# Second batch's attention residual: added by an accumulating load instead of by VectorE

## The chip, the cores and the metric

The kernel runs on one core of one Trainium2 chip. The metric is device time in microseconds for one execution. A core has five engines that each work through their own queue in order and wait for one another by semaphores: TensorE (PE; its weight loads are shown as PEld), VectorE (DVE), ScalarE (ACT), GpSimd (POOL) and SyncE (SP). Transfers are issued from the SP, ACT and GpSimd queues and carried out by 16 DMA engines.

## The reference

Input x is (4 batches, 512 times, 128 features f, 64 channels h), float32; d = f * h = 8192. Layer 0, cut to its formulas:

```python
xn = layernorm(x.reshape(b, t, d), ln_attn_g, ln_attn_b)
k, v, r = xn @ Wk, xn @ Wv, sigmoid(xn @ Wr)          # 64 states each
states = scan over t of  s = decay * s + k_t * v_t
x = x + ((r * states) @ Wo).reshape(b, t, f, h)       # attention, its residual
xn = layernorm(x.reshape(b, t, d), ln_freq_g, ln_freq_b).reshape(b, t, f, h)
x = x + gelu(convolution over f of xn, 3 taps, h -> h, + freq_b)
xn = layernorm(x.reshape(b, t, d), ln_time_g, ln_time_b)
to = causal depthwise convolution over t of xn, 3 taps, + time_b
x = x + layernorm(to, time_ln_g, time_ln_b)
x = x + gelu(x @ ffn_W1 + ffn_b1) @ ffn_W2 + ffn_b2   # over h
```

Layer 1 takes a moving average over t (25 wide) as trend, transforms the rest over t, mixes 128 modes by complex weights per channel, transforms back and adds the trend. The change touches the lines of the attention and the convolution over f alone, and for one of the four batches.

## The kernel before

Layer 0 keeps one batch as 64 chunks of 128 rows of d (two f times 64 h) by 512 times. Two chunks make a pair, so a batch has 32 pairs (`NPR`), and a pair is a tile of 128 partitions by 2 x 512 float32, 512 KB. Five stages run for each batch: `project` (k, v, r and the statistics of the first layernorm), `scan`, `attend_and_convolve`, `convolve_time`, and `feed_forward`.

TensorE's order is written by hand: each stage is a generator that issues a piece and yields its weight, and `in_turn` steps two generators alternately by their share of progress. Its table puts the attention and convolution over f of batch 1 beside the convolution over t of batch 0. The other engines' orders come from the framework's scheduler, which also sets the semaphore waits; every queue is then in order. A tile from a pool is a rotating buffer: a new tile of a tag waits until the old holder's readers are done.

`attend_and_convolve(b)` works by pairs in a loop over i. Step i does these pieces:

- `attend(i)`: SP loads the pair of x into xp (L295, in `load_x`) and a block of Wo (L525). TensorE multiplies Wo by r * states into the one PSUM tile of tag "a" (L529). VectorE adds xp to it, which gives x1 (L531, 3 buffers of tag "x1"), and multiplies x1 by the second layernorm's scale, which gives z (L535, 4 buffers).
- `convolve(i - 2)`: TensorE starts with the constant part (L550), then the neighbouring chunks of z (L559; so it needs z of the pair after it), then the chunks themselves (L564). ScalarE applies gelu in PSUM (L565), VectorE adds x1, which gives x2 (L567), GpSimd issues the store of x2 to memory (L568), ScalarE squares x2 (L570) and makes the convolution's weights two pairs ahead (L543).
- `add_up(i - 3)`: TensorE sums x2 and its square over d (L252, into st), for the third layernorm.

`convolve_time(0)`, which runs beside it, takes per pair: a load of x2 from SP (L612), VectorE's multiply and subtract (L613, L616), on ScalarE the first tap of two chunks (L621), on VectorE the four other taps (L625), on GpSimd a correction of two columns (L631) and the store of the result (L632), on ScalarE its square (L672), on TensorE the sums (L252, into p).

Tags "xp" and "x1" have three buffers each. `spare(tag, n)` gives a tile of a tag in the same pool.

Of the kernel before, what the change touches and what calls it, by code (L numbers as in the profile page):

```python
# [10 lines left out]
F32 = mybir.dt.float32  # L11
AF = mybir.ActivationFunctionType
ALU = mybir.AluOpType
# [3 lines left out]
P = 128  # L17
# [5 lines left out]
SL = 512  # L23
NS = D // SL
NPR = NCH // 2
# [55 lines left out]
def layer0(ctx, tc, dram, x, xt, vecs, wkvr, wo, wdec, wconv, fbias, w1, fb1, w2, fb2, x4):  # L81
# [4 lines left out]
    nc = tc.nc  # L86
# [7 lines left out]
    fr = ctx.enter_context(tc.tile_pool(name="fr", bufs=3))  # L94
# [10 lines left out]
    def two(pool, tag):  # L105
        return pool.tile([P, 2, SL], F32, tag=tag, name=tag)
# [54 lines left out]
    def neighbours(q, c):  # L161

        return (c - 1, q), (c + 1, 1 - q)

    def rows_of(q, d):

        return 1 - q if d < 0 else q
# [79 lines left out]
    def add_up(st, i, pair, squares, first, last):  # L247

        for j in range(2):
            for k, src in ((0, pair), (1, squares)):  # L250
                q = 2 * j + k
                nc.tensor.matmul(  # L252
                    st[32 * q : 32 * q + 32, :], lhsT=ones, rhs=src[:, j, :],
                    start=first, stop=last,
                )

    def finish(st, bank, tag):

        s_sb = rowp.tile([P, SL], F32, tag="s", name="s_sb")
        nc.scalar.copy(s_sb, st)  # L260
        yield CHAIN
        pm = bank()
        for t in range(NT):
            nc.tensor.matmul(
                pm[:, 2 * t : 2 * t + 2], lhsT=s_sb[:, t * P : (t + 1) * P], rhs=pick,
                start=True, stop=True,
            )
        me = tiny.tile([P, NT, 2], F32, tag=f"me{tag}", name="me")
        nc.vector.tensor_copy(me.rearrange("p t k -> p (t k)"), pm[:, 0 : 2 * NT])
        return me[:, :, 0], me[:, :, 1]  # L270

    def moments(mean, square, tag):

        var, rs, mrs = cols(f"var{tag}"), cols(f"rs{tag}"), cols(f"mrs{tag}")
        nc.vector.tensor_tensor(var, mean, mean, ALU.mult)
        nc.vector.tensor_tensor(var, square, var, ALU.subtract)
        rsqrt(rs, var)
        nc.vector.tensor_tensor(mrs, mean, rs, ALU.mult)
        return rs, mrs

    def rows(bank, a, b, names):
        both = rowp.tile([P, 2, SL], F32, tag=names, name=names)
        for k, col in enumerate((a, b)):
            pb = bank()
            spread(pb, col)
            nc.scalar.copy(both[:, k, :], pb)  # L286
            yield CHAIN
        return both[:, 0, :], both[:, 1, :]

    def pair_of(row):  # L290
        return row.unsqueeze(1).to_broadcast([P, 2, SL])

    def load_x(b, i):
        xp = fr.tile([P, 2, SL], F32, tag="xp", name="xp")
        nc.sync.dma_start(xp, xt[b, 2 * i : 2 * i + 2].rearrange("c p t -> p c t"))  # L295
        return xp

    def spare(tag, n):
        return fr.tile([P, 2, n], F32, tag=tag, name=tag, bufs={"z": 4, "wx": 2}.get(tag, 3))

    def c_bank():
        return two(ps_c, "c")
# [212 lines left out]
    def attend_and_convolve(b):  # L515
        rst, rs, mrs = scanned.pop(b)
        rb, mb = yield from rows(of_a, rs, mrs, "rm4" if b == 1 else "rm")

        nc.vector.tensor_scalar(mb, mb, at_one[:, 1:2], at_one[:, 0:1], ALU.mult, ALU.add)
        x1s, zs, ws, waiting = {}, {}, {}, {}  # L520

        def attend(i):
            xp = load_x(b, i)
            wo_sb = fr.tile([P, P], F32, tag="wo", name="wo_sb")
            nc.sync.dma_start(wo_sb, wo[:, i, :])  # L525
            at = two(ps_a, "a")
            for j in range(2):
                js = slice(j * S, (j + 1) * S)
                nc.tensor.matmul(at[:, j, :], lhsT=wo_sb[js, :], rhs=rst[js, :], start=True, stop=True)  # L529
            x1 = x1s[i] = fr.tile([P, 2, SL], F32, tag="x1", name="x1")  # L530
            nc.vector.tensor_tensor(x1, at, xp, ALU.add)  # L531
            z = fr.tile([P, 2, SL], F32, tag="z", name="z", bufs=4)
            for j in range(2):
                zs[2 * i + j] = z[:, j, :]
            nc.vector.tensor_tensor(z, x1, pair_of(rb), ALU.mult)  # L535

        def scaled(i):

            wcs = fr.tile([P, 2, P + H], F32, tag="wcs", name="wcs")
            for j in range(2):  # L540
                c = 2 * i + j
                ws[c] = wcs[:, j, :]
                nc.scalar.mul(wcs[:, j, :], wc_sb[:, i % 2, :], vec[:, G2, c : c + 1])  # L543

        def convolve(i):
            cv = c_bank() if i % 2 or held[0] else two(ps_m, "m")
            for h in range(2):
                for j in range(2):
                    q = 32 * (2 * h + j)
                    nc.tensor.matmul(  # L550
                        cv[h * H : (h + 1) * H, j, :], lhsT=cgr[q : q + 2, i, :], rhs=mb[q : q + 2, :],
                        start=True, stop=False,
                    )
            for j in range(2):
                c = 2 * i + j
                for n, h in neighbours(i % 2, c):
                    if 0 <= n < NCH:
                        rs = halves[rows_of(n // 2 % 2, n - c)]
                        nc.tensor.matmul(  # L559
                            cv[halves[h], j, :], lhsT=ws[n][rs, P:], rhs=zs[n][rs, :], start=False, stop=False  # L560
                        )
            for j in range(2):
                c = 2 * i + j
                nc.tensor.matmul(cv[:, j, :], lhsT=ws[c][:, 0:P], rhs=zs[c], start=False, stop=True)  # L564
            nc.scalar.activation(cv, cv, AF.Gelu_apprx_tanh)  # L565
            x2 = two(bk, "x2")
            nc.vector.tensor_tensor(x2, cv, x1s.pop(i), ALU.add)  # L567
            nc.gpsimd.dma_start(x2d[b][2 * i : 2 * i + 2].rearrange("c p t -> p c t"), x2)  # L568
            sq2 = bk.tile([P, 2, SL], F32, tag="sq", name="sq2")
            nc.scalar.activation(sq2, x2, AF.Square)  # L570
            for c in (2 * i - 2, 2 * i - 1):
                zs.pop(c, None)
                ws.pop(c, None)
            if i + 2 < NPR:
                scaled(i + 2)
            waiting[i] = x2, sq2

        for i in range(NPR + 3):

            while begin[attend_and_convolve] < b + (min(i, 3) - 3) / 4:  # L580
                yield BLOCKED
            if i < 2:
                scaled(i)
            if i < NPR:
                attend(i)
                yield 1.0
            if 1 < i < NPR + 2:
                convolve(i - 2)
                yield 5.0
            while i == 3 and feeding[0]:  # L590
                yield BLOCKED
            if i == 3:
                st = ps_s.tile([P, SL], F32, tag="s", name="st")
                free_s[0] = False
            if i > 2:
                add_up(st, i - 3, *waiting.pop(i - 3), i == 3, i == NPR + 2)
                yield 1.0
            if b == 0 and i >= NPR and i < NPR + 2:
                begin[attend_and_convolve] = b + (0.25 if i == NPR else 0.75)
        begin[attend_and_convolve], free_s[0] = b + 1, True  # L600
        mean3, sq3 = yield from finish(st, of_a, 3)
        carried[b] = moments(mean3, sq3, 3)
# [248 lines left out]
    def nothing(b):  # L851
        yield 1.0

    J, Z, A, C, O, F = project, scan, attend_and_convolve, convolve_time, open_feed, feed_forward
    begin[A] = 0
    needed = {A: scanned, C: carried, O: causal, F: opened}
# [340 lines left out]
```

## Time and profile before

| | us |
|---|---|
| median of 3 runs | 3745.81 (3739.15 to 3752.97) |
| the profiled execution | 3734.79 |
| its span, first to last instruction | 3733.0 |

Busy time over the span: PE 3521.2 us (94%), DVE 2671.9 (72%), ACT 1778.0 (48%), POOL 447.3 (12%). The shares differ by stage. Three stretches ahead of the stage that the change touches, from the same view:

| stretch, us | what runs | PE | DVE | ACT | POOL | DMA share |
|---|---|---|---|---|---|---|
| 200 to 300 | batch 0 attention, batch 1 project | 94.7 | 53.4 | 24.2 | 6.6 | 0.70 |
| 300 to 400 | the same | 97.7 | 53.4 | 29.7 | 8.0 | 0.73 |
| 400 to 511 | its end, with batch 1's scan | 106.5 | 63.6 | 45.3 | 12.2 | 0.55 |

In the profile a line reads: engine, line of the kernel, operation, tile written <- tiles read, shape. "Idle before" is time in which an engine waited, with what ended the wait. The time from issue to landing of a transfer is given for those from GpSimd. TensorE's ends are modelled, so a busy TensorE is not one at its peak.

### The profile page before, as it was taken

What the parts mean: (1) busy time and instruction counts of PE and PEld (TensorE: products, weight loads), DVE (VectorE), ACT (ScalarE), POOL (GpSimd) and SP (SyncE); (2) the same over time, 40 slices, a digit from 0 to 9 for tenths busy, and PEclk for the clock granted to TensorE, in tenths of its full rate; (3) what the DMA queues carried; (4) which work ended last, traced back from release to release, by engine and by line L of the source; (5) the groups of instructions that cost most, each with busy time, mean ns of one, the idle gap of its engine ahead of it and who ended that gap; (6) DMA issues with size and microseconds to landing.
All of it is one profiled execution on the core that took longest, in us unless ns stands there. A gap on an engine that the chain in (4) does not pass through costs nothing. (4 is left out here: it accounts for less than half of the span.)

```text
span 3733.0 us, 53000 instructions
## 1 busy us (share of the span) xinstructions
PE 3521.2 (94%) x20041; PEld 1360.6 (36%) x20041; DVE 2671.9 (72%) x3498; ACT 1778.0 (48%) x2331; POOL 447.3 (12%) x654
## 2 busy tenths in 40 slices
PE   9999999999998999999989989999989999989998
PEld 4433322234333223433322233333323843328533
DVE  4455569976776896676789699946658277792677
ACT  0012346655656565565656578868854200152100
POOL 0000012210101221001122122100000000001000
PEclk9999999999999999999999999999999999999999
DMA  9867657787874687788578677645569478894687
GB/s 314 279 211 242 227 177 262 260 276 265 290 262 168 235 280 271 266 292 278 182 238 286 213 247 267 234 149 196 198 203 287 150 240 290 290 297 164 213 294 260
DMA packets 427223, 910.29 MB, mean 244 GB/s; under 512 B 32728, under 2 KB 83160, under 8 KB 422872
## 3 DMA queue, kind: packets, MB, share of 16 engines
q1 hardware_dynamic: 353136, 636.92, 52.5%
q0 software_dynamic: 71680, 268.46, 19.7%
q8 instruction: 160, 2.62, 0.3%
q10 hardware_dynamic: 2152, 1.51, 0.1%
q14 instruction: 95, 0.78, 0.1%
HBM read 638.26 MB, written 268.50 MB: 243 GB/s over the span
## 5 line engine op out<-in xcount | busy, mean ns | idle before, releaser
L745 PE MATMUL p<-mid,w_sb 64*64 64x512 f32 x2048 | 554.5, 599 | 20.3 <-DVE wx L758 20.3
L745 PE MATMUL pb<-mid,w_sb 64*64 64x512 f32 x2048 | 536.2, 598 | 0.0
L737 ACT ACTIVATE mid<-c,fb_sb 128x1024 f32<-128x1024 f32 x256 | 284.3, 1111 | 97.2 <-PE c L732 94.8
L737 ACT ACTIVATE mid<-m,fb_sb 128x1024 f32<-128x1024 f32 x256 | 284.6, 1112 | 93.5 <-PE m L732 92.1
L732 PE MATMUL c<-x,w_sb 64*64 64x512 f32 x2016 | 281.2, 611 | 13.2 <-ACT mid L737 6.9
L732 PE MATMUL m<-x,w_sb 64*64 64x512 f32 x2016 | 283.0, 612 | 6.7 <-ACT ob L777 4.9
L745 PEld LDWEIGHTS p<-mid,w_sb 64*64 64x64 f32 x2048 | 155.5, 135 | 294.9 <-issue 262.0
L409 PE MATMUL a<-xp,wx 128*128 128x512 f32 x512 | 242.6, 617 | 9.1 <-DVE wx L358 8.6
L1043 ACT COPY two<-a 128x512 f32<-128x512 f32 x64 | 37.5, 585 | 428.9 <-PE a L1038 428.9
L1066 PE MATMUL b<-xin,avg_sb 128*128 128x512 f32 x512 | 230.8, 593 | 3.3 <-DVE xin L1072 3.3
L1072 DVE TENSOR_TENSOR xin<-b,pm 128x512 f32<-128x512 f32 x256 | 159.1, 683 | 100.2 <-PE b L1069 85.3
L570 ACT ACTIVATE sq<-x 128x1024 f32<-128x1024 f32 x128 | 135.1, 1055 | 181.4 <-DVE x L567 181.3
L625 DVE SCALAR_TENSOR_TENSOR to<-kd,vec,to 128x510 f32<-128x510 f32 (+1 forms) x272 | 197.1, 744 | 9.8 <-ACT to L621 8.7
L700 ACT ACTIVATE kd<-kd,vec 128x512 f32<-128x512 f32 x256 | 192.8, 803 | 3.1 <-DVE kd L692 3.1
L252 PE MATMUL st<-x,ones 128*32 128x512 f32 x512 | 176.8, 603 | 13.1 <-DVE x L567 13.1
L925 DVE COPY xf<-b 128x256 f32<-128x256 f32 x128 | 54.4, 425 | 178.3 <-PE b L1012 169.4
L625 DVE SCALAR_TENSOR_TENSOR z<-x,vec,z 128x511 f32<-128x511 f32 x240 | 175.9, 745 | 5.3 <-ACT z L621 3.0
L531 DVE TENSOR_TENSOR x<-a,xp 128x1024 f32<-128x1024 f32 x128 | 156.1, 1220 | 30.6 <-PE a L529 28.4
L703 DVE TENSOR_TENSOR x<-kd,kx 128x1024 f32<-128x1024 f32 x126 | 154.1, 1223 | 32.8 <-ACT kd L700 32.7
L529 PE MATMUL a<-rst,wo_sb 64*128 64x512 f32 x512 | 147.0, 648 | 27.1 <-DVE x L531 25.1
L758 DVE SCALAR_TENSOR_TENSOR x4t<-p,fb_sb,x 128x512 f32<-128x512 f32 x64 | 47.9, 748 | 172.0 <-PE pb L745 169.6
L692 DVE TENSOR_TENSOR kd<-kd,rm 128x1024 f32<-128x1024 f32 x128 | 155.7, 1220 | 7.8 <-ACT rm L286 6.3
(269 smaller groups left out, 6755.1 us busy)
## 6 DMA issues: line engine op xcount, KB each, us to landing
xp<-in_xt SPq DMA_DIRECT2D x256, 512.0 KB
kh<-to SPq DMA_DIRECT2D x156, 512.0 KB
x<-x POOLq DMA_DIRECT2D x128, 512.0 KB, 4.6
kx<-x SPq DMA_DIRECT2D x128, 512.0 KB
x<-ob POOLq DMA_DIRECT2D x64, 1024.0 KB, 8.0
xin<-x SPq DMA_DIRECT2D x64, 1024.0 KB
out<-xin POOLq DMA_DIRECT2D x64, 1024.0 KB, 6.6
x<-x SPq DMA_DIRECT2D x96, 512.0 KB
```

The costliest lines, as they stand in the source:

```text
L252: nc.tensor.matmul(st[32 * q : 32 * q + 32, :], lhsT=ones, rhs=src[:, j, :], start=first, stop=last,)
L409: nc.tensor.matmul(pa[:, k, :], lhsT=wq[:, j, k * P : (k + 1) * P], rhs=xp[:, j, :], start=first and j == 0, stop=last and j == 1,)
L531: nc.vector.tensor_tensor(x1, at, xp, ALU.add)
L625: tap = nc.vector.scalar_tensor_tensor(to[:, j, k:], xr[:, j, : SL - k], vec[:, w, c], to[:, j, k:], ALU.mult, ALU.add)
L692: nc.vector.tensor_tensor(d, d, pair_of(mb), ALU.subtract)
L700: tc.keep_in_program_order(nc.scalar.activation(d[:, j, :], d[:, j, :], AF.Identity, bias=vec[:, B4, c], scale=vec[:, G4, c]))
L703: nc.vector.tensor_tensor(x3, d, x2, ALU.add)
L732: nc.tensor.matmul(pm[halves[j], h, :], lhsT=w1_sb[halves[h], q * H : (q + 1) * H], rhs=x3[halves[h], j, :], start=True, stop=True,)
L737: nc.scalar.activation(mid, pm, AF.Gelu_apprx_tanh, bias=fb1_sb[:, q : q + 1])
L745: nc.tensor.matmul(sums2[i][j][halves[h], :], lhsT=w2_sb[halves[j], q, :], rhs=mid[halves[j], h, :], start=q == 0, stop=q == 3,)
L1066: nc.tensor.matmul(po[j], lhsT=avg_sb[:, j, :], rhs=xin[:, j, :], start=True, stop=False)
L1072: nc.vector.tensor_tensor(by_n(xin[:, j, :]), by_n(po[j]), by_c(pm[j % 2][:, j // 2, :]), ALU.add)
```

## The change

For batch 1 alone (`by_dma`), `attend` doesn't load x into xp. ScalarE copies the attention from PSUM into x1, and GpSimd issues a load of the same 512 KB of x that adds to x1 as it lands (`accum_op=ALU.add`). VectorE's addition L531 is not issued for these 32 pairs. The tiles x1 are taken in turn from the tags "x1" and "xp", so that six buffers serve them. The convolution over f follows three pairs behind the attention (`late = 3`) instead of two, and the sums four behind; the loop has one more step. The other batches keep the code they had, with `late = 2`.

```diff
+        by_dma = b == 1
+        late = 3 if by_dma else 2
+
         def attend(i):
-            xp = load_x(b, i)
+            if not by_dma:
+                xp = load_x(b, i)
             wo_sb = fr.tile([P, P], F32, tag="wo", name="wo_sb")
             nc.sync.dma_start(wo_sb, wo[:, i, :])
             at = two(ps_a, "a")
             for j in range(2):
                 js = slice(j * S, (j + 1) * S)
                 nc.tensor.matmul(at[:, j, :], lhsT=wo_sb[js, :], rhs=rst[js, :], start=True, stop=True)
-            x1 = x1s[i] = fr.tile([P, 2, SL], F32, tag="x1", name="x1")
-            nc.vector.tensor_tensor(x1, at, xp, ALU.add)
+            x1 = x1s[i] = spare("xp" if by_dma and i % 2 else "x1", SL)
+            if by_dma:
+                nc.scalar.copy(x1, at)
+                nc.gpsimd.dma_start(x1, xt[b, 2 * i : 2 * i + 2].rearrange("c p t -> p c t"), accum_op=ALU.add)
+            else:
+                nc.vector.tensor_tensor(x1, at, xp, ALU.add)
             z = fr.tile([P, 2, SL], F32, tag="z", name="z", bufs=4)
...
-        for i in range(NPR + 3):
+        for i in range(NPR + late + 1):
...
-            if 1 < i < NPR + 2:
-                convolve(i - 2)
+            if late <= i < NPR + late:
+                convolve(i - late)
                 yield 5.0
...
-            if i > 2:
-                add_up(st, i - 3, *waiting.pop(i - 3), i == 3, i == NPR + 2)
+            if i > late:
+                add_up(st, i - late - 1, *waiting.pop(i - late - 1), i == late + 1, i == NPR + late)
                 yield 1.0
```

## The prediction, made before the changed kernel ran

> **What bounds the kernel now.** I first read the busy windows by stage, since the chain of waits reaches only back to 1969 us and so says nothing of this stage (the second batch's attention and convolution over f, beside the first batch's convolution over t). The columns are stretch, length, busy us and count of PE, PEld, DVE, ACT and POOL, then clock, DMA share and GB/s:
>
> ```profile
> 511.00:537.00 26.00, 22.23 (x119) 7.09 (x114) 17.27 (x18) 8.96 (x13) 3.44 (x5) 1.00 0.53 175
> 537.00:789.00 252.00, 231.17 (x1168) 54.66 (x1160) 250.27 (x271) 155.85 (x214) 70.50 (x92) 1.00 0.77 262
> 789.00:815.00 26.00, 22.99 (x84) 10.40 (x84) 9.25 (x22) 4.76 (x7) 3.95 (x7) 0.87 0.80 281
> ```
>
> From 537 to 789 us VectorE has 250.3 of 252 us: it sets this stage, and only there. PE's 231 is no second limit; the waits view has PE stopping in this stage for DVE's results (30.5 us for L531, 30.1 for L567). The same window for L531 alone, the addition that leaves VectorE:
>
> ```profile
> 537.00:789.00 252.00, 32.85 (x27) 1.00 0.77 262
> ```
>
> Then the timelines of one step, since the added work makes a round between four in-order queues:
>
> ```profile
> 642.45 1.21 DVE L567 TENSOR_TENSOR x<-m,x 128x1024 f32<-128x1024 f32 x1
> 643.59 1.21 DVE L616 TENSOR_TENSOR kd<-kd,rm 128x1024 f32<-128x1024 f32 x1
> ...
> 645.85 1.21 DVE L531 TENSOR_TENSOR x<-a,xp 128x1024 f32<-128x1024 f32 x1
> 646.99 0.73 DVE L625 SCALAR_TENSOR_TENSOR to<-kd,vec,to 128x511 f32<-128x511 f32 x1
> ```
>
> ```profile
> 643.70 1.06 ACT L570 ACTIVATE sq<-x 128x1024 f32<-128x1024 f32 x1
> ...
> 652.82 1.04 ACT L570 ACTIVATE sq<-x 128x1024 f32<-128x1024 f32 x1
> 653.77 1.04 ACT L672 ACTIVATE sq<-to 128x1024 f32<-128x1024 f32 x1
> ```
>
> The reader should take start-to-start times: an L531 or L567 holds VectorE 1.14 us, a tap (L625) 0.66, or 0.74 if the next one needs it; the square L570 starts 1.25 after the start of its L567 and ScalarE is free 0.95 later. Last, GpSimd's two pieces and the price of the copy:
>
> ```profile
> L568 POOL DMA_DIRECT2D x<-x x29: 725/725/734, 549.0 to 788.5; - x29
> DMA to landing us min/median/max: 3.2/4.7/8.1
> ```
>
> ```profile
> L631 POOL TENSOR_TENSOR to<-to,vec x31: 192/1048/1842, 545.7 to 785.7; 128x4 f32<-128x4 f32 x31
> ```
>
> ```profile
> L415 ACT COPY kvrg<-m x1: 1012/1012/1012, 443.4 to 443.4; 128x1024 f32<-128x1024 f32 x1
> ```
>
> A 512 KB transfer from GpSimd lands 4.7 us after its issue in this stage. A load of that size from SP (L351) is issued at 472.17 us and ends VectorE's wait at 476.76, so about 4.6 us too.
>
> **What the Trainium skill says.** "DMA: Bandwidth & Descriptors", section "Anatomy of one DMA — SWDGE (gpsimd) path", prices such a transfer at 2.0 us plus bytes over 436 GB/s: 3.2 us for 512 KB. The trace's shortest, 3.2, agrees; the load of this stage adds 1.5. The same page, "Rules for kernel authors", says that an accumulating DMA reads its destination and writes it later; no run here shows one. "SBUF — State Buffer", section "Who interferes with whom", says that a VectorE instruction with two SBUF inputs contends with a GpSimd instruction that reads SBUF; the spread of L631, 0.19 to 1.84 us for four elements a partition, fits that.
>
> **The change part by part.** Taken away: 27 L531 in the full stretch, 27 x 1.14 = 30.8 us of VectorE (five more lie before it, where VectorE has gaps), and 32 loads of xp on SP. Those loads moved 512 KB each, as the accumulating ones do, so plain traffic stays. A step (one pair of both stages) takes (769.81 - 539.55) / 26 = 8.86 us from L531 to L531; VectorE alone could then do it in 7.72.
>
> Added on ScalarE: 32 copies of 1.01 us. It has 155.9 of 252 us; with 27 more it stays far from full: nothing by itself. Added on GpSimd: 32 issues of 0.73 (the price of L568) over 70.5 of 252 busy: nothing by itself. The PSUM bank of the attention is freed by the copy instead of L531, no later in the step.
>
> What costs is the new chain copy, issue, landing, z (L535). The built program's order on each engine, which holds no time, shows for nearly every pair q of the stage:
> - VectorE: x2 of q-4 (L567), four taps (L625), L613, L616, z of q, x2 of q-3.
> - ScalarE: square of x2 of q-4 (L570), second L621 of the step, copy of q.
> - GpSimd: L631, which waits for the third tap, then the accumulating load of q.
>
> So z of q stands ahead of x2 of q-3, while its load is issued only after x2 of q-4 in the same step. The extra pair of delay helps TensorE, which needs z two steps later, but VectorE waits at z in order, and behind it stand x2, the taps, and through them the next load. One round, from the start of x2: square starts at 1.25, L621 at 2.20 and ends 0.80 later, so the third tap, which needs it, starts at 3.05 and ends at 3.8 (the copy, at 2.9 to 3.9, is not later). L631 at its mean of 0.86 (page of groups in this stage), 0.48 from its end to the next issue (774.33 to 774.81 in GpSimd's timeline) and 0.05 for the signal: issue at 5.2. Then the landing L, then 1.14 for z. Round = 6.3 + L.
>
> L is the unknown. From below: a plain transfer's shortest, 3.2. From above: its longest, 8.1. Nearest value: 4.7, plus up to 1.2 if the destination's 512 KB are read in series at the rate of the page above (an estimate). I take half of that, L = 5.3. Round: 11.6 us, 3.9 more than VectorE's 7.72.
>
> By the order, 14 of the pairs 6 to 31 have just one tap, L613 and L616 between trigger and z: 14 x 3.9 = 54.6. Five have a further tap there: 5 x 3.2 = 16.0. Two (14 and 15) have the load ahead of L631 and 6.6 us of work in between, and pair 23 has 5.4: about 1.1 each, 3.3. Four (6, 7, 8, 24) have over 7 us of it: nothing. Stalls: 74 us.
>
> Start of the stage: loads 4 and 5 stand behind the stores of x2 of pairs 0 and 1, and z and the next x2 right behind them on VectorE. Before, those three x2 start at 522.63, 527.64 and 535.52. After: x2 of the first batch's last pair ends at 511.9, store and load issue 0.8 later, landing 518.0, z of 0 and 1 to 520.4, convolution and gelu (1.1 + 2.0 + 1.0) give x2 at 524.6; twice 1.25 + 0.8 + 5.3 + 1.14 on top give 541.6. The first batch's convolution over t, which began at 537.3, waits behind it: +5.5, less 1.1 for one z more done by then.
>
> Sum: 5.5 - 1.1 - 30.8 + 74 = +48 us. The later stages are only moved. On the profiled execution (span 3733.0, 3734.79 in all) that gives 3783; the median of the runs is 11 us higher, 3745.81, and I predict on that: 3794.
>
> **Rivals.** The sum moves by some 25 us for each us of L (22 rounds and three landings at the start).
> - Faster: z finds x1 landed and VectorE's relief is passed on. At L = 2.5 the sum is 48 - 2.8 x 25 = -22, so 3724; it decides below L = 3.4, where the sum is zero. For it: VectorE full, and short L631 (0.19) would shift the point up by 0.7. Against it: no plain transfer in this stage is below 3.2.
> - Relief and stalls cancel: L near 4.0, the median landing of L632: 48 - 33 = +15, 3761. For it: L632's own number. Against: the extra read.
> - The accumulation is dear: L = 7.5, 48 + 55 = +103, 3849. For it: stores of 8.1 us occur and the destination is read; against: DMA share 0.77 leaves room, and a longer step lowers it.
> - The extra step of the convolution makes the stage longer by itself: VectorE has the same work then, and no L531 in it; under 3 us either way, inside the others.
>
> **How the numbers follow.** A measurement here tells about 0.5%, 19 us, from no change. Forecast (L from 4.2 to 6.8, +19 to +85): 0.60. Dear (beyond +85): 0.18. Cancelling (within 19): 0.13. Faster: 0.09. So faster 0.09, same 0.13, slower 0.78. The range reaches from L = 3.0 (-10) to L = 7.6 (+106): 3736 to 3852, which leaves out most of the faster case and the upper half of the dear one.
>
> **What would show it.** Right: in the changed profile VectorE is busy well under 90% in the stage, idle before z because of a DMA from in_xt, with some 10 to 12 us from z to z; L531's successor no longer stops PE; landings of the new load at 4 to 7 us. The stage ends near 836 instead of 789. Wrong: VectorE still at 99%, z waiting for nothing, and the stage 25 to 30 us shorter; or a stall before L567 or in PE with z on time. A landing under 3.4 us would overturn the sign, a landing over 7 only the size.

## The result, and the profile after

| | before | after |
|---|---|---|
| median, us | 3744.91 (4 runs, 3739.15 to 3752.97) | 3839.00 (4 runs, 3830.28 to 3842.79) |
| span of the profiled execution, us | 3733.0 | 3836.7 |
| last x2 (L567) of the first batch starts, us | 510.67 | 516.02 |
| first multiplication (L613) of the convolution over t starts, us | 537.27 | 557.23 |
| statistics at the end of the second batch's stage (L269), us | 794.52 | 894.39 |

After over before is 1.0246 (95%: 1.022 to 1.0272), so the change costs 94 us. All of it arises in the stage that the change touches: from the first batch's last x2 to the statistics 283.9 us before and 378.4 after, +94.5. The 5.3 us by which that last x2 comes later lie ahead of the stage, and 3.8 more lie behind it (2942.3 us from the statistics to the end of the span instead of 2938.5); the runs of one kernel scatter by more than that, 13 us, so neither is laid to the change.

The lines have moved: L535 (z) is now L543, L567 (x2) L575, L568 L576, L570 L578, L613 L621, L616 L624, L621 L629, L625 L633, L631 L639, L632 L640. New are L536, the copy, and L537, the accumulating load.

First the busy windows from the first L613 (now L621) to the statistics; of the kernel before for VectorE alone (stretch, length, VectorE's busy time and count, clock, DMA share, GB/s), of the kernel after with all engines in the order used above:

```profile
537.20:794.50 257.30, 252.52 (x274) 0.99 0.77 264
```

```profile
557.20:894.30 337.10, 256.92 (x1158) 58.13 (x1150) 231.86 (x247) 179.32 (x242) 99.13 (x119) 0.90 0.71 202
```

VectorE is busy 20.7 us less, with 27 instructions fewer, and idle 105.2 us instead of 4.8. No other engine is full: PE has 257 of 337, and its granted clock falls to 0.90. The waits view of VectorE in the same stretch (us in total, times, longest) names the idle time:

```profile
DVE z L543 <- DMA xp<-in_xt: 44.3, 11, 5.9
DVE z L543 <- DMA x<-in_xt: 42.7, 13, 4.9
DVE to L633 <- ACT to L629: 8.5, 21, 0.9
DVE z L543 <- PE p L252: 5.0, 2, 3.5
```

24 of the 26 z in it wait for the accumulating load, 3.6 us each and 87.0 in all. The load itself, from the view of its line over the whole run (durations ns min/median/max):

```profile
L537 POOL DMA_DIRECT2D x<-in_xt x16: 1194/1226/1291, 518.3 to 849.2; - x16
...
DMA to landing us min/median/max: 5.5/6.4/9.9
```

It lands 6.4 us after its issue begins, and GpSimd needs 1.23 us to issue it. Both are more than for the plain transfers of the same 512 KB shown above (4.7 and 0.73).

One round can be followed in the timelines of VectorE, ScalarE and GpSimd (start, duration, engine, line; in brackets the idle time before it and what ended it):

```profile
628.18 1.22 DVE L575 TENSOR_TENSOR x<-m,x 128x1024 f32<-128x1024 f32 x1
...
631.23 1.53 DVE L633 SCALAR_TENSOR_TENSOR to<-kd,vec,to 128x511 f32<-128x511 f32 x2 [0.39 <-ACT to L629]
...
638.44 1.23 DVE L543 TENSOR_TENSOR z<-x,rm 128x1024 f32<-128x1024 f32 x1 [3.16 <-DMA x<-in_xt]
```

```profile
629.43 1.06 ACT L578 ACTIVATE sq<-x 128x1024 f32<-128x1024 f32 x1 [5.70 <-DVE x L575]
630.40 0.80 ACT L629 ACTIVATE to<-kd,vec 128x512 f32<-128x512 f32 x1
631.10 0.99 ACT L536 COPY x<-a 128x1024 f32<-128x1024 f32 x1
```

```profile
632.12 0.70 POOL L639 TENSOR_TENSOR to<-to,vec 128x4 f32<-128x4 f32 x1 [1.69 <-issue]
632.77 1.22 POOL L537 DMA_DIRECT2D x<-in_xt  x1
```

The x2 at 628.18, itself right behind a z that had waited 3.40, releases the square (629.43), behind which stands the first tap L629 (630.40), which the third tap on VectorE needs (631.23); L639 waits for that tap, and the load stands behind L639 (632.77). It ends z's wait at 638.44, with x2 1.14 later. So a round has 4.59 us to the issue, 5.67 to z and 1.14 to x2. Over the 26 z of the stage the time from one z to the next is 12.0 us on average; from x2 to the issue 4.6 is the usual value, and the median from issue to landing is 6.4.

The start of the stage, in the same view of VectorE, with three of its waits for the first loads:

```profile
524.17 1.23 DVE L543 TENSOR_TENSOR z<-x,rm 128x1024 f32<-128x1024 f32 x1 [6.93 <-DMA x<-in_xt]
528.98 1.23 DVE L543 TENSOR_TENSOR z<-xp,rm 128x1024 f32<-128x1024 f32 x1 [3.59 <-DMA xp<-in_xt]
...
545.50 1.22 DVE L543 TENSOR_TENSOR z<-x,rm 128x1024 f32<-128x1024 f32 x1 [7.26 <-DMA x<-in_xt]
```

From the first batch's last x2 to the first L621 it takes 41.2 us (516.02 to 557.23); before it took 26.6.

### The profile page after: what moved, and what is told of

It is laid out like the page before. It is cut to its first block, busy times and chain, and to the rows that moved or that the text cites. A ratio compares the mean times of both kernels' runs of the same rounds, so it can differ in the third digit from the quotient of the medians.

```text
span 3836.7 us, 52995 instructions
## 1 busy us (share of the span) xinstructions
PE 3559.6 (93%) x20041; PEld 1366.6 (36%) x20041; DVE 2645.6 (69%) x3466; ACT 1805.5 (47%) x2363; POOL 480.5 (13%) x686
## 5 line engine op out<-in xcount | busy, mean ns | idle before, releaser
L578 ACT ACTIVATE sq<-x 128x1024 f32<-128x1024 f32 x128 | 135.1, 1056 | 303.5 <-DVE x L575 303.4
L252 PE MATMUL st<-x,ones 128*32 128x512 f32 x512 | 188.9, 640 | 78.5 <-DVE x L575 78.5
L633 DVE SCALAR_TENSOR_TENSOR to<-kd,vec,to 128x511 f32<-128x511 f32 (+1 forms) x272 | 198.6, 746 | 18.9 <-ACT to L629 16.3
L543 DVE TENSOR_TENSOR z<-x,rm 128x1024 f32<-128x1024 f32 x112 | 136.7, 1221 | 63.3 <-DMA x<-in_xt 58.5
L576 POOL DMA_DIRECT2D x<-x x128 | 93.8, 733 | 687.6 <-DVE x L575 648.8
L633 DVE SCALAR_TENSOR_TENSOR z<-x,vec,z 128x511 f32<-128x511 f32 x240 | 175.6, 744 | 5.3 <-ACT z L629 3.0
L533 PE MATMUL a<-rst,wo_sb 64*128 64x512 f32 x512 | 156.5, 686 | 21.3 <-DVE x L539 14.3
```

The lines of the kernel that those rows point to most:

```text
L252: nc.tensor.matmul(st[32 * q : 32 * q + 32, :], lhsT=ones, rhs=src[:, j, :], start=first, stop=last,)
L633: tap = nc.vector.scalar_tensor_tensor(to[:, j, k:], xr[:, j, : SL - k], vec[:, w, c], to[:, j, k:], ALU.mult, ALU.add)
```

## The experiments

Ratios are to the kernel before, run beside each experiment on the same chip, with their 95% intervals.

**Is it the third pair of delay, or the buffers?** The kernel before, with x1 in six buffers, x loaded by SP into x1 itself, VectorE's addition kept, and the convolution three pairs behind:

```diff
-            xp = load_x(b, i)
...
+            x1 = x1s[i] = spare("xp" if by_dma and i % 2 else "x1", SL)
+            if by_dma:
+                nc.sync.dma_start(x1, xt[b, 2 * i : 2 * i + 2].rearrange("c p t -> p c t"))
+                nc.vector.tensor_tensor(x1, at, x1, ALU.add)
```

> SP loads x into the tile of x1 (the tags taken in turn, as in the change) and VectorE adds the attention in place; the convolution stays three pairs behind. No copy, no accumulating load. Theory (z waits in VectorE's queue for the landing of its own step's load): VectorE has the work of before and no such wait, so within 10 us of before, about 3745, and no wait of z for a DMA. Rival (the longer delay costs by itself, through buffers or the extra step): 15 us or more over before.

Measured: 3743.35 us, ratio 1.0016 (1.0003 to 1.003). The later convolution with the six buffers costs some 6 us by itself (1 to 11), and no z in it waits for a DMA.

**And is the third pair what protects the change?** The change with `late = 2`:

```diff
-        late = 3 if by_dma else 2
+        late = 2
```

> The copy and the accumulating load as in the change, the convolution two pairs behind as before. Theory: VectorE's order has z of pair q ahead of the x2 of its step here too, with the same three or four instructions between the trigger of the load and z, so the delay is without effect: within 15 us of the changed kernel's 3839. Rival (three pairs are what lets z wait less): clearly slower than 3839, by 30 us or more.

Measured: 3847.63 us, ratio 1.0294 (1.0274 to 1.0313), 18 us above the change by the ratios and 9 by the medians, where the theory had 15 at most. The added pair helps a little; it doesn't take the round apart, since z still stands ahead of the x2 in question.

**What is the accumulation worth?** The change with a plain load in the same place of GpSimd's queue:

```diff
-                nc.gpsimd.dma_start(x1, xt[b, 2 * i : 2 * i + 2].rearrange("c p t -> p c t"), accum_op=ALU.add)
+                nc.gpsimd.dma_start(x1, xt[b, 2 * i : 2 * i + 2].rearrange("c p t -> p c t"))
```

> The load from GpSimd doesn't accumulate: it overwrites the copy, so batch 1's attention residual is left out of the result. All instructions, their order and their waits are those of the changed kernel. Theory: the round is the same but L falls from 6.4 us to that of a plain transfer, 4.2 to 4.7, which on some 25 rounds is 40 to 55 us less than 3839: 3784 to 3800, still slower than before. Rival (accumulating costs nothing beside a plain load; what is late is the queue): within 12 us of 3839.

Measured: 3777.99 us, ratio 1.0108 (1.0087 to 1.0128). The view of its load's line:

```profile
L537 POOL DMA_DIRECT2D x<-in_xt x16: 722/727/731, 516.5 to 795.2; - x16
...
  DVE z L543: 60.8, 29
...
DMA to landing us min/median/max: 3.7/4.6/7.7
```

In the same place a plain load lands in 4.6 us and is issued in 0.73: adding costs 1.8 us from the issue's start to the landing, and the issue's record is 0.5 longer. That is 52 us of the time by the ratios (1.0246 less 1.0108, of 3740), or 29 us for each us of landing; the forecast had 25. Copies, issues and the round alone still leave the kernel 1.1% slower than before. So the round makes the change slow, and the accumulation more than doubles its price.

**Does the round hang on z's place?** z of a pair is taken one place later in VectorE's order, held behind the newest x2; the rest is the change:

```diff
+        def normalise(i):
...
+            by_rb = nc.vector.tensor_tensor(z, x1s[i], pair_of(rb), ALU.mult)
+            if by_dma and "x2" in newest:
+                behind(by_rb, newest["x2"])
...
+            if by_dma and 0 < i <= NPR:
+                normalise(i - 1)
```

> The convolution stays three pairs behind as in the change, but VectorE takes z of a pair one place later, behind the x2 whose store goes just ahead of that pair's load, so that some 7.4 us of other VectorE work instead of about 1.8 stand between the trigger of the load and z. Theory (a round x2, copy, issue, landing, z with one x2 per round): the issue comes 4.6 after the trigger, the load lands 6.4 later, 11.0 in all, and 7.4 plus up to 2 us of it are covered, so a round is about 9.5 us instead of 11.4 to 11.7: 3765 to 3785 us where before has 3740, waits of z for a load 1 to 3 us each. Rival (the load gets slower as the step gets shorter, DMA engines being full): waits stay above 3 us each and the time above 3800. Rival (any place behind the newest x2 is enough): no waits in the steady stretch, 3735 to 3745.

Measured: 3759.89 us, ratio 1.0037 (1.0022 to 1.0051), 5 us below the theory's band (11 by the ratio, on 3740), and outside both rivals'. VectorE's waits in its stage:

```profile
DVE z L553 <- DMA x<-in_xt: 23.9, 12, 7.7
...
DVE z L553 <- DMA xp<-in_xt: 13.1, 8, 2.8
```

20 waits, 37.0 us, 1.9 each: the load, with the same accumulation and a landing of 6.6 us, is now covered for the most part. One place in an in-order queue was worth 2.1% of the run.

**And two places later?** The same with four pairs of delay and `normalise(i - 2)`:

> z of pair q is made two steps after its load is given out, held behind the newest x2 in VectorE's order, and the convolution is four pairs behind; copy and accumulating load as in the change. Theory: some 15 us of VectorE's work now lie between the trigger of a load and its z, more than the 4.6 + 6.4 us of the path, so the waits of z vanish in the steady stretch, VectorE is full again with 1.14 us less for each pair, and only the start of the stage still costs 5 to 15 us: 3720 to 3735, 10 to 25 us under before. Rival (the accumulating loads or the copies themselves slow the stage, through DMA, GpSimd or ScalarE): at or over before, 3745 to 3790, with VectorE under 95% busy.

Measured: 3733.05 us, ratio 0.9985 (0.9975 to 0.9996). Its windows, with the columns as above, and VectorE's timeline of one step:

```profile
511.00:540.00 29.00, 22.59 (x85) 6.32 (x84) 8.64 (x10) 11.88 (x14) 10.21 (x11) 0.81 0.83 172
...
680.00:720.00 40.00, 36.40 (x186) 9.06 (x184) 39.21 (x42) 30.08 (x41) 18.63 (x20) 1.00 0.95 273
```

```profile
700.06 1.22 DVE L587 TENSOR_TENSOR x<-m,x 128x1024 f32<-128x1024 f32 x1
...
702.33 2.98 DVE L647 SCALAR_TENSOR_TENSOR to<-kd,vec,to 128x511 f32<-128x511 f32 x4
705.34 1.23 DVE L635 TENSOR_TENSOR kd<-x,rm 128x1024 f32<-128x1024 f32 x1
706.60 1.22 DVE L638 TENSOR_TENSOR kd<-kd,rm 128x1024 f32<-128x1024 f32 x1
707.74 1.22 DVE L587 TENSOR_TENSOR x<-c,xp 128x1024 f32<-128x1024 f32 x1
```

The loss is gone: VectorE is full again, and a steady step takes 7.68 us (700.06 to 707.74). Not all steps are like it: from z to z the mean is 8.10 us over 26 steps, where it was 8.88 before. The time lies in the band of 3720 to 3735, but the gain is 6 us by the ratio, less than the 10 expected at least, where the addition was worth 30.8. I first put that down to the start of the stage, where the first windows show VectorE at 8.6 of 29 us.

**Is it the start?** Three kernels. The change with the first six pairs on the old path (SP's load, VectorE's addition):

```diff
+            early = by_dma and i < 6
...
+            if early:
+                nc.sync.dma_start(x1, xt[b, 2 * i : 2 * i + 2].rearrange("c p t -> p c t"))
+                nc.vector.tensor_tensor(x1, at, x1, ALU.add)
+            elif by_dma:
```

> The change as it is, with the first six pairs on the old path alone: it takes the start of the stage out of the loss and leaves the rounds. Theory: the accumulating loads cost some 10 to 14 us at the start (first taps of the convolution over t at 557 us against 543 where they would be without), so 10 to 14 us less than the change: 3817 to 3825 us where before has 3740, and the rounds stay at 11.4 to 11.7 us. Rival (the start costs the 4.4 us of the forecast, and the rest of the delay there comes from elsewhere): 3826 to 3832.

Measured: 3839.61 us, ratio 1.0253 (1.0232 to 1.0273): no gain on the change. In its trace the stretch from the first batch's last x2 to the first L613 is 33.9 us, 7.3 less than in the change, and the stretch after it 2.7 longer. The theory's 10 to 14 us aren't there; 4.6 are in the profile, none in the medians, and the time fits the rival's band no better.

The same edit on the kernel with z two places later:

> z two places later as in the kernel with four pairs of delay, and the first six pairs of the stage on the old path (a load from SP, the addition on VectorE). Theory: what held that kernel to a gain of 6 us was the start of the stage, 10 to 15 us of waits for the first accumulating loads; VectorE has room there, so these go: 3715 to 3728 us where before has 3740. Rival (the start is set by what TensorE and GpSimd do at the turn of the stages, or the DMA engines at a share of 1.0 set the stage): 3730 to 3737, no gain over the kernel with all 32 pairs on the new path.

Measured: 3736.14 us, ratio 0.9989 (0.9979 to 0.9999): no better than with all 32 pairs on the new path, as the rival had it. In its trace the start takes 31.3 us (518.78 to 550.08), against 33.9 with all 32 pairs (508.99 to 542.93) and 26.6 before.

And the whole old schedule for six pairs (z at once, convolution two pairs behind), then a change to the new one, with two steps that have no convolution:

```diff
+        def due(i):
+            k = i - 2 if i <= EARLY else i - late
+            return k if 0 <= k < NPR and not (by_dma and EARLY < i < EARLY + 3) else None
```

> The first six pairs run as in the kernel before (load from SP, addition on VectorE, z at once, convolution two pairs behind), and only from the seventh on are the accumulating load, z two places later and four pairs of delay used; the delay is made up by two steps without a convolution. Theory: the kernels with four pairs of delay from the first pair on win some 25 to 30 us of VectorE's time in the steady stretch and lose some 15 to 20 of it at the start, where the convolution over t begins later or starves; with the old start that loss goes, and the stage ends 15 to 25 us earlier than before: 3716 to 3727 us where before has 3740. Rival (the DMA engines at a share near 1.0, or TensorE, hold the stage as it is): 3730 to 3740, waits of VectorE for other things in the steady stretch.

Measured: 3733.45 us, ratio 0.9988 (0.9975 to 1.0001). The convolution over t now begins as early as before (26.6 us after the first batch's last x2). The two empty steps give some of it back, with VectorE at 31.8 of 40 us in the window from 560 to 600. This too is in the rival's band. By the ratios the three starts end within 2 us of each other, with intervals of some 4 us either way. In the traces the stage takes 278.0 us with all 32 pairs on the new path, 274.6 with six early pairs and 274.4 with the old start, where before has 283.9. So an old start brings back some 3.5 us, which these medians can't show and which is far less than the theory's 15 to 20; with the two empty steps, part of what is saved at the start is lost again behind it (247.8 us from the first multiplication to the statistics instead of 244.0).

**Where is the rest?** The stretch from the first L613 to the statistics shows it, for z two places later (columns as for VectorE above):

```profile
542.90:787.00 244.10, 230.59 (x249) 0.98 0.96 280
```

It is 13.2 us shorter than before (257.3). By VectorE's starts in the two traces, 27 additions less give 30.7 us. The taps, L613 and L616, as many as before, take 10.3 more (7.2, 2.8 and 0.3). Waits take 6.1 more, 5.6 of them one wait of x2 for ScalarE's gelu at 550.89, and one x2 more falls into the stretch, 1.1. With the 7.3 us that the start is longer, 5.9 us of gain are left, which is what the ratio shows. So what is missing is mostly of two kinds: 13 us of the start and the first wait after it, of which the kernels above brought back 3.5, and 10 us of slower neighbours on VectorE.

In the timeline above L635 and L638, which works on its result, start 1.26 us apart, and any other two neighbours of that size 1.14. Four taps and the step to L635 take 3.01 us. In each chunk the second tap adds to what the first wrote; such a pair, shown as 1.53 us in the change's round above, starts 0.78 apart. Beside VectorE's addition (the first experiment's kernel, same view) the taps stand apart:

```profile
642.66 1.41 DVE L633 SCALAR_TENSOR_TENSOR to<-kd,vec,to 128x510 f32<-128x510 f32 x2
643.98 1.22 DVE L621 TENSOR_TENSOR kd<-x,rm 128x1024 f32<-128x1024 f32 x1
645.12 1.22 DVE L575 TENSOR_TENSOR x<-m,x 128x1024 f32<-128x1024 f32 x1
646.25 1.22 DVE L624 TENSOR_TENSOR kd<-kd,rm 128x1024 f32<-128x1024 f32 x1
```

Two taps there take 1.32 us, 0.66 each, and L624 stands 2.27 after L621 with work in between. In the trace an instruction that waits for the one just before it has 0.03 to 0.04 us of idle time ahead of it. The full stretch has 17 of these before, 9 in the first experiment's kernel, which keeps the addition, and 92 and 94 in the change and with z two places later. So they come with the addition's leaving VectorE; why the scheduler's order then puts them side by side, no run shows. The Trainium skill ("Perfetto Trace Analysis", section "DVE / Act Engine Instruction (TENSOR_ADD, Activation, etc)") says that the end which the profile shows is when the write is acknowledged and the semaphore sent. That agrees: an independent follower starts 0.08 before the end that is shown (1.14 against 1.22), a dependent one 0.03 after it.

So I took the taps in another order in the kernel with z two places later, the first tap of each chunk and then the second of each:

```diff
-            for k, w in ((1, W1), (2, W0)):
+        for k, w in ((1, W1), (2, W0)):
+            for j in range(2):
+                c = slice(2 * i + j, 2 * i + j + 1)
...
+                elif b == 0 and j == 0 and k == 2:
+                    behind(tap, second)
...
+            if by_dma and first_tap[0] is not None:
+                behind(by_rb, first_tap[0])
```

> The kernel with four pairs of delay and z two places later, with VectorE's four taps of a pair of the first batch taken in another order: the first tap of each chunk, then the second of each, so that no tap reads what the one just before it wrote. Theory (without the addition in between, instructions that depend on each other stand side by side on VectorE, and each such neighbour costs about 0.08 us more, which is why a steady step is 7.68 us and not about 7.3): a tap goes from 0.745 us to about 0.67 from start to start, the steady step to about 7.4, and the run 6 to 8 us below the same kernel without it: 3724 to 3731 us where before has 3740. Rival (the second chunk's first tap on ScalarE is late for the new order): VectorE waits for ScalarE before a tap, the step stays at 7.7 and the time at 3731 to 3738.

Measured: 3726.55 us, ratio 0.9957 (0.994 to 0.9974), the fastest kernel of this study, 0.4% under the one before. The timeline of a step of it:

```profile
647.41 1.22 DVE L639 TENSOR_TENSOR kd<-x,rm 128x1024 f32<-128x1024 f32 x1
...
652.08 2.85 DVE L653 SCALAR_TENSOR_TENSOR to<-kd,vec,to 128x511 f32<-128x511 f32 x4
654.97 1.23 DVE L639 TENSOR_TENSOR kd<-x,rm 128x1024 f32<-128x1024 f32 x1
```

The taps take 2.89 us instead of 3.01 and the step 7.56 instead of 7.68: the direction is shown, the size is half of the expected. The rival holds for the other half, as a line of ScalarE's timeline shows:

```profile
652.02 0.80 ACT L647 ACTIVATE to<-kd,vec 128x512 f32<-128x512 f32 x1
```

This is the second chunk's first tap. It ends at 652.82, and VectorE's second tap, which needs it, starts at 652.86, 0.78 after the one before, as late as a dependent one. In the stretch 46 instructions now stand right behind a VectorE instruction that they wait for, instead of 94, but 17 taps behind ScalarE. Some 28 steps of 0.12 are 3.4 us. The ratios differ by 0.28%, 10 us; the two kernels were not run side by side, their intervals nearly touch (0.9975 and 0.9974), and the new order of the taps is in all four batches' code, though held in place for the first alone. So the rest isn't explained.

## Why the prediction was right, and where its size was off

It said slower, 3794 us and a stage 48 us longer, by a round of x2, issue, landing and z. The stage became 94.5 us longer by that round. Point by point:

- **VectorE bounds the stage, and so only there can relief be had.** Right: the kernel with z two places later, whose z waits are gone in the steady stretch, has VectorE at 39 of 40 us again, with a steady step of 7.68. The forecast's 7.72 was a mean over 26 steps, though, and the mean there is 8.10: the relief was not passed on whole.
- **Copies and issues cost nothing by themselves.** Not refuted: the kernels with all 32 of both and z placed later aren't slower than the one before. No run had them alone.
- **The round and z's place in it.** Right, and shown twice: a shorter landing in the same place takes the ratio from 1.0246 to 1.0108, and moving z alone by one place takes it to 1.0037.
- **The landing L = 5.3 us.** This term was the most wrong: at 25 us for each us of L, the 1.1 us by which 6.4 exceeds it are 27 us. The forecast took a plain landing and half of an estimated serial read of the destination, 0.6 us. Measured in the same place, the accumulation adds 1.8, more than the 1.2 of the whole read. The rule of "DMA: Bandwidth & Descriptors", section "Rules for kernel authors", that an accumulating DMA reads its destination and writes it later, agrees in direction. From x2 to the issue it was 4.6 us instead of 5.2, which took about half of it back: from z to z 12.0 us where 11.6 was forecast.
- **The stalls, 74 us.** z's waits for the load are 87.0 us, 24 of them where the forecast had four pairs without any: +13.
- **Left out: waits other than z's.** The third tap's waits for ScalarE's L629 (8.5, before 0.9) and z's for PE (5.0) are stalls that the sum did not have: +13.
- **The relief, 30.8 us.** VectorE's busy time fell by 20.7: +10. The forecast gave a tap 0.74 us where the next one needs it (it is 0.78), but took all other instructions to cost what they had cost, and put the change of neighbours at nothing. Now 75 more of them stand right behind one that they wait for, and each loses about 0.08 us of overlap: some 6 us, an estimate. The other 4 are the ends of instructions before a wait, which nothing overlaps any more.
- **The start, 5.5 less 1.1 us.** Between the first batch's last x2 and the first L621 it was 14.6 us: +10. The forecast had the first loads landed by 518.0; GpSimd issued the first six at 518.27, 522.08, 524.31, 526.55, 539.30 and 548.92 us. The kernel with six early pairs on the old path shows, though, that taking half of this away, a net 4.6 us of its trace, doesn't show in the median.

13, 13, 10 and 10 on top of 48 are 94, which is what was measured; the later stages are only moved, as forecast. All four are on the same side; only inside the first did one error, the earlier issue, hide part of another, L. The 94 us lie beyond the +19 to +85 to which the forecast gave 0.60, among the sums over +85 that it gave to the dear accumulation, at 0.18. That rival came nearest (3849 us), but at L = 6.4 and not 7.5, a landing that the forecast's own band of 4.2 to 6.8 holds: 23 of the 46 us of excess, the waits other than z's and the relief, came from terms that neither had.

## What to carry to other kernels

When work leaves a full in-order engine for a transfer, look up what that engine does between the instruction that triggers the transfer and the one that consumes it. If that is less than the landing, the consumer's wait holds back the next trigger. More delay of the work behind it hardly helps (9 to 18 us here); moving the consumer one or two places back in its queue does. Before counting the freed time as gain, see whether others, without the removed instruction, come to stand right behind ones that they wait for.

## What the runs showed of the hardware

- An accumulating load of 512 KB from GpSimd into SBUF lands after 6.4 us (5.5 at the least) where a plain one in its place lands after 4.6 (3.7). Its issue is recorded with 1.23 us on GpSimd instead of 0.73, but the next instruction of that queue can start before this ends: in the kernel with z two places later L653 starts at 705.05, 0.78 after the load at 704.27.
- A transfer issued right behind it is late too. The store of the convolution over t (L632, now L640), from the views of its line in the stage before and after:

```profile
DMA to landing us min/median/max: 3.2/4.0/5.5
```

```profile
L640 POOL DMA_DIRECT2D to<-to x31: 727/1199/1262, 570.6 to 888.9; - x31
DMA to landing us min/median/max: 3.2/8.1/10.6
```

  It lands in 8.1 us instead of 4.0, and its own issue is recorded with 1.20. Behind the plain load of the third experiment it lands in 5.4, with 0.73, so 1.4 of the 4.1 us are there without the accumulation and 2.7 come with it. Nothing waited for it here.
- On VectorE an instruction that waits for the one just before it starts 0.12 us later than another: 1.26 against 1.14 for 128x1024, 0.78 against 0.66 for a tap. That holds where it reads the result (L638 after L635) and where it writes over what the other has just read (L635 after the last tap). With z two places later the full stretch has 77 more of these than before, some 9 us (an estimate, 77 by 0.12).
